# Graph attention and gated graph network, one core: the copies of the GRU's aggregates out of PSUM move from VectorE to ScalarE, and the planner makes the order anew

## The chip, the core and the metric

The kernel runs on one core of a Trainium2 chip. The metric is the device time of one execution in microseconds (us); lower is better. Before the change it is 2776.41 us, the median of 3 runs (2775.74 to 2777.18).

## The reference

There are 128 independent graphs of 128 nodes with 256 features each, all in float32. Three graph attention layers are followed by a gated graph network of three GRU steps. Every layer normalizes its input, applies a ReLU and adds its result to the input.

```python
# layers 0, 1, 2
h = relu(layernorm(x))
Wh = h @ W                                   # 256 x 256 weights
e = leaky_relu((Wh @ a1)[:, :, None] + (Wh @ a2)[:, None, :], 0.2)
att = softmax(where(adj > 0, e, -9e15), axis=-1)
x = x + elu(att @ Wh)
# layer 3, on h = relu(layernorm(x))
A = (adj != 0)
for i in range(3):
    m = h @ weight[i]
    aggr = einsum('bst,bsd->btd', A, m)      # sum over the neighbours
    gi, gh = aggr @ w_ih.T + b_ih, h @ w_hh.T + b_hh
    r = sigmoid(i_r + h_r); z = sigmoid(i_z + h_z)
    n = tanh(i_n + r * h_n)
    h = (1 - z) * n + z * h
x = x + h
```

## The kernel before, in words

**Groups.** The 128 graphs are cut into 33 groups: one of 2 graphs, 31 of 4 and one of 2 (`SIZES`). For each group `gat(g)` does the three attention layers (`attention(g, l, ...)`) and prepares the GRU, and `gru(g, ...)` does the three steps. Most tiles of a 4-graph group are 128 partitions x 512 columns.

**Attention.** For a layer, VectorE takes statistics (`bn_stats` L413, `bn_aggr` L415), GpSimd the power for the reciprocal root (L422, L424), and ScalarE makes the normalized rows `xn` (L497). VectorE forms the scores (L505), GpSimd prepares the next sum `xo` from `xt` (L516), VectorE adds and masks the scores (`em`, L547), applies the leaky ReLU (L559) and takes the row maxima (`nmx`, L561). ScalarE takes the exponentials (L565), VectorE the reciprocals (L572), scales (L576) and transposes in blocks (`tr_at`, L441); the rest of the transposition goes through DRAM by DMAs from SyncE's queue (L448, L452). TensorE multiplies (`ahp`, L617), ScalarE copies out of PSUM (`ah`, L624), TensorE multiplies with the weights (`hp`, L636), ScalarE takes the exponential (`t`, L650), and VectorE adds both parts into `xo` (L652, L654). The first two groups transpose on TensorE and not through DRAM (L536, L589).

**One GRU step.** `step(i)` has two halves `c` of 128 features. The message weights are folded with the input weights into `wc`, so that the step first sums the neighbours' states and then multiplies. `aggregate(k)`, for each half `k` of the features, multiplies the states `hn[k]` (nodes on partitions) with the adjacency `am` into the PSUM tile `agp` (L803; 4 products, one for each graph) and copies `agp` to the SBUF tile `ag[k]` (L811). `half(c)` accumulates in PSUM: `nn`, `r` and `z` from the state `h` and `whh`, then `r`, `ni` and `z` from `ag` and `wc` (all L780). ScalarE reads them: `wn` (L833), `r` (L838), `n` (L848), `z` (L853). VectorE combines them: L841, L846, `d` (L861 or L863, and L867), and the new state (L870). For the next step the new state must lie with nodes on partitions: for groups 2 to 30 `turned_state` transposes blocks on VectorE (L466) and turns them through DRAM (L469, L473); the other groups transpose on TensorE (`hnp`, L752) and copy on ScalarE (`hn`, L792).

**PSUM.** Eight banks of 128 x 512: two for attention, five for the GRU's `nn`, `r`, `z` and `ni`, and one, `tr`, for `agp`, `hnp` and `hTp`. As there is one `tr` bank, the next `agp` or `hnp` can't begin before the copy of the last has read it.

**What sets the order.** Nothing is issued where it stands in the code. Every operation goes into a `Plan` with an engine, a cost and a rank (`add`, L62). `issue` (L108) plays the program through with these costs, as a list scheduler: on each engine it takes, of the operations that could start within 0.1 us of the first, the one of lowest rank, among those within `AHEAD` = 6 ranks of the oldest operation that is still open. The order so found is fixed as the instruction order of each engine; each engine then works its list in that order and waits where an input isn't there. The costs are functions of the column count (L256 to L266): `dve` is 0.12 + cols / 1000, `act` is 0.25 + cols / 1400. Loads and stores by DMA are planned on SyncE with 0.45 us each and a landing time. The plan allows for neither a VectorE operation that is held up by GpSimd nor a DMA that lands later than planned. The rank of the GRU's element-wise work, the aggregates' copies among it, is 2 lower than its step's (`quick`, L767), so that it goes ahead of the attention's.

Of the kernel before, what the change touches and what calls it, by code (L numbers as in the profile page):

```python
# [39 lines left out]
class Plan:  # L40
# [21 lines left out]
    def add(self, engine, cost, rank, fn, reads=(), writes=(), after=(), takes=()):  # L62


        reads = [k if isinstance(k, tuple) else (k, None) for k in reads]
        writes = [k if isinstance(k, tuple) else (k, None) for k in writes]
        vals = list(dict.fromkeys(v for v, _ in reads + writes))
        vals += [v for v in dict.fromkeys(takes) if v not in vals]
        op = Op(engine, cost, rank, fn, vals)
        for v in vals:  # L70
            v.ops.append(op)

        def others(book, key):
            for part, ops in book.get(key[0], {}).items():
                if part is None or key[1] is None or part == key[1]:
                    yield from ops

        for key in reads:
            for d in others(self.writers, key):
                op.deps[d] = True  # L80
        for key in writes:
            for book in (self.writers, self.readers):
                for d in others(book, key):
                    op.deps.setdefault(d, False)
        for d in after:
            op.deps.setdefault(d, False)
        for v, part in writes:
            w, r = self.writers.setdefault(v, {}), self.readers.setdefault(v, {})
            if part is None:
                w.clear()  # L90
                r.clear()
            else:
                r.pop(part, None)
            w[part] = [op]
        for v, part in reads:
            if (v, part) not in writes:
                self.readers.setdefault(v, {}).setdefault(part, []).append(op)
        for d in op.deps:
            d.users.append(op)
        self.ops.append(op)  # L100
        return op
# [80 lines left out]
def kernel(  # L182
# [25 lines left out]
    nc = tc.nc  # L208
# [25 lines left out]
    add, load = plan.add, plan.load  # L234
# [15 lines left out]
    def bank(tag, name):  # L250
        n = BANKS[tag]
        return plan.val(
            psum, tag, n, lambda: psum.tile([P, T], FT, tag=tag, name=name, bufs=n)
        )

    def pe(cols):  # L256
        return 0.035 + cols / 600 if cols <= P else 0.01 + cols / 600

    def dve(cols):
        return 0.12 + cols / 1000  # L260

    def act(cols):
        return 0.25 + cols / 1400
# [462 lines left out]
    def gru(g, xt, am, hn0, h0):  # L726
# [3 lines left out]
        TG = n_g * N  # L730
# [17 lines left out]
        def node_major(name, hv, k, rank, to):  # L748
            ps = bank("tr", f"hnp_{name}_{k}")

            def turn(b):
                add("PE", 0.11, rank, lambda: nc.tensor.transpose(  # L752
                    ps.t[:, b * P : (b + 1) * P], hv.t[:, b * P : (b + 1) * P], ident
                ), reads=[hv], writes=[(ps, b)], takes=[to])

            for b in range(n_g):
                turn(b)
            return ps
# [4 lines left out]
        def step(i):  # L763
# [3 lines left out]
            quick = rank - URGENT  # L767
# [18 lines left out]
            def aggregate(k):  # L786

                if i > 0:
                    hv = hn[k]
                    if not through:  # L790
                        hp = node_major(name, h[k], k, rank + 0.1 * k, hv)
                        add("ACT", act(TG), quick, lambda: nc.scalar.copy(  # L792
                            hv.t[:, :TG], hp.t[:, :TG]), reads=[hp], writes=[hv])
                ps = bank("tr", f"agp_{name}_{k}")
                t = ag[k]

                def part(b):
                    def fn():
                        if i > 0:
                            s = hv.t[:, b * P : (b + 1) * P]  # L800
                        else:
                            s = hn0.t[:, b, k * P : (k + 1) * P]
                        nc.tensor.matmul(  # L803
                            ps.t[:, b * P : (b + 1) * P], s, am.t[:, b, :], start=True, stop=True
                        )
                    add("PE", pe(P), rank + 0.1 * k, fn,
                        reads=[hv if i > 0 else hn0, am], writes=[(ps, b)], after=after, takes=[t])

                for b in range(n_g):
                    part(b)  # L810
                add("DVE", dve(TG), quick, lambda: nc.vector.tensor_copy(t.t[:, :TG], ps.t[:, :TG]),  # L811
                    reads=[ps], writes=[t])

            def half(c):
# [7 lines left out]
                for k in range(KD):  # L822
                    early = rank + 0.1 * k if c == 0 else at
                    ops = [
                        product(nn, cn, whh, h[k], k, k == 0, k == KD - 1, early, takes),
                        product(pr, cr, whh, h[k], k, k == 0, False, early, takes),
                        product(pz, cz, whh, h[k], k, k == 0, False, early, takes),
                    ]
                    if k == 0:
                        begun += ops  # L830
                    if c == 0:
                        aggregate(k)
# [125 lines left out]
```

## Time and profile before

| | |
|---|---|
| median of the runs | 2776.41 us |
| profiled execution | 2774.5 us |
| its span | 2772.7 us, 32377 instructions |
| TensorE matmul busy | 2710.1 us (98%) |
| VectorE busy | 2199.0 us (79%), 5738 instructions |
| ScalarE busy | 1171.7 us (42%), 2511 instructions |
| GpSimd busy | 288.2 us (10%) |
| copies of the aggregates, L811, on VectorE | 198, 130.8 us |
| copies of `ah`, L624, on ScalarE, of the same shapes | 198, 112.9 us |

The profile was taken in an execution of its own, which is 1.9 us below the median of the runs. PE is TensorE's matmuls and PEld its weight loads, DVE is VectorE, ACT is ScalarE, POOL is GpSimd and SP is SyncE. A float32 product appears as two matmul records. The records' ends are modelled, so that the busy time of PE says how often it had work and not how fast it worked; the distance from start to start tells that. "idle before" is the time that an engine stood still ahead of an instruction, and the name after the arrow is what released it last.

### The profile page before, as it was taken

Reading aid. Unit: us, or ns where it says so; the run is one execution under the profiler, and the core shown is the slowest. Engines: PE = TensorE matmul, PEld = TensorE weight load, DVE = VectorE, ACT = ScalarE, POOL = GpSimd, SP = SyncE. Lnnn points to the kernel's source line nnn. Section 1 sums busy time; section 2 is a strip of 40 time slices with the busy share of each in tenths; the row PEclk is TensorE's granted clock in tenths of the full one; section 3 lists DMA queues with packets and bytes.
Section 4 is the critical chain, followed back from the end, with each engine's and each line's share of the span. In section 5 each row is a group of like instructions: output and inputs, shape, how many; then the busy total and the mean of one; then the engine's idle time right before and its main releaser. Section 6 shows DMA issues by size and latency. Waiting matters only on the chain.

```text
span 2772.7 us, 32377 instructions
## 1 busy us (share of the span) xinstructions
PE 2710.1 (98%) x9557; PEld 1565.2 (56%) x9557; DVE 2199.0 (79%) x5738; ACT 1171.7 (42%) x2511; POOL 288.2 (10%) x369
## 2 busy tenths in 40 slices
PE   6998999999999999999999999999999999999998
PEld 4755555555555555555555555555555555555546
DVE  7778888887888878887888878788788887888644
ACT  4444444443444444443444444444344444444322
POOL 2101011010101010101011101011101010101000
PEclk9999999999999999999999999999999999999999
DMA  3213234333334323334333334333333333333310
GB/s 102 57 44 103 77 94 110 103 86 92 89 93 111 105 75 99 91 92 111 97 83 96 95 92 107 103 84 91 88 100 103 104 87 88 80 94 93 78 44 12
DMA packets 503519, 246.08 MB, mean 89 GB/s; under 512 B 280624, under 2 KB 472112, under 8 KB 503344
## 3 DMA queue, kind: packets, MB, share of 16 engines
q1 hardware_dynamic: 503344, 244.03, 33.6%
q8 instruction: 76, 1.25, 0.2%
q14 instruction: 99, 0.81, 0.1%
HBM read 140.06 MB, written 103.87 MB: 88 GB/s over the span
## 4 chain that ended last, share of the span: by engine, by line
PE 84%; DVE 11%; ACT 2%; DMA 1%; issue 1%; SPq 0%; POOL 0%; ACTq 0%; DVEq 0%; POOLq 0%
PE r L780 21%; PE z L780 21%; PE ni L780 11%; PE hp L636 10%; PE nn L780 9%; PE ahp L617 6%; PE agp L803 5%; DVE em L547 2%; DVE xo L652 1%; DVE xo L654 1%; ACT em L565 1%; DVE ag L811 1%; DVE d L867 1%; DVE h L870 1%; DVE d L863 1%
## 5 line engine op out<-in xcount | busy, mean ns | idle before, releaser
L780 PE MATMUL nn<-h,whh 128*128 128x512 f32 (+1 forms) x792 | 396.3, 582 | 11.2 <-DMA h<-d_h 9.0
L780 PE MATMUL r<-ag,wc 128*128 128x512 f32 (+1 forms) x792 | 394.5, 581 | 8.4 <-DVE ag L811 8.4
L780 PE MATMUL r<-h,whh 128*128 128x512 f32 (+1 forms) x792 | 395.2, 580 | 0.0
L780 PE MATMUL z<-h,whh 128*128 128x512 f32 (+1 forms) x792 | 394.3, 579 | 0.0
L780 PE MATMUL z<-ag,wc 128*128 128x512 f32 (+1 forms) x792 | 394.1, 579 | 0.0
L780 PE MATMUL ni<-ag,wc 128*128 128x512 f32 (+1 forms) x792 | 394.0, 579 | 0.0
L636 PE MATMUL hp<-w,ah 128*128 128x256 f32 x1536 | 360.5, 380 | 2.5 <-ACT ah L624 2.4
L636 PEld LDWEIGHTS hp<-w,ah 128*128 128x128 f32 x1536 | 290.5, 191 | 100.7 <-issue 61.5
L841 DVE SCALAR_TENSOR_TENSOR n<-r,wn 128x512 f32<-128x512 f32 (+1 forms) x198 | 133.6, 675 | 224.8 <-ACT r L838 222.9
L505 DVE SCALAR_TENSOR_TENSOR scr<-xn,va 128x256 f32<-128x256 f32 x732 | 268.6, 419 | 32.4 <-ACT xn L497 32.2
L833 ACT ACTIVATE wn<-nn,bh 128x512 f32<-128x512 f32 (+1 forms) x198 | 132.9, 671 | 359.1 <-PE nn L780 358.9
L838 ACT ACTIVATE r<-r,brz 128x512 f32<-128x512 f32 (+1 forms) x198 | 132.8, 671 | 351.8 <-PE r L780 351.5
L803 PEld LDWEIGHTS agp<-am,hn 128*128 128x128 f32 x1536 | 201.1, 191 | 88.3 <-issue 64.1
L780 PEld LDWEIGHTS r<-ag,wc 128*128 128x128 f32 x792 | 148.3, 190 | 176.4 <-issue 145.8
L780 PEld LDWEIGHTS z<-h,whh 128*128 128x128 f32 x792 | 150.1, 190 | 170.9 <-issue 161.5
L565 ACT ACTIVATE em<-em,nmx 128x128 f32<-128x128 f32 x384 | 149.3, 390 | 228.3 <-DVE nmx L561 228.3
L780 PEld LDWEIGHTS z<-ag,wc 128*128 128x128 f32 x792 | 148.3, 190 | 159.4 <-issue 157.4
L780 PEld LDWEIGHTS r<-h,whh 128*128 128x128 f32 x792 | 147.8, 191 | 159.7 <-issue 155.0
L780 PEld LDWEIGHTS ni<-ag,wc 128*128 128x128 f32 x792 | 146.7, 190 | 154.5 <-issue 137.1
L617 PEld LDWEIGHTS ahp<-at,xn 128*128 128x128 f32 x1536 | 188.8, 194 | 47.6 <-issue 42.1
L803 PE MATMUL agp<-am,hn 128*128 128x128 f32 x1536 | 205.9, 276 | 8.7 <-ACT hn L792 4.4
L780 PEld LDWEIGHTS nn<-h,whh 128*128 128x128 f32 x792 | 138.5, 191 | 103.8 <-issue 95.0
(91 smaller groups left out, 3401.9 us busy)
## 6 DMA issues: line engine op xcount, KB each, us to landing
d_hn<-tr_hn SPq DMA_DIRECT2D x116, 256.0 KB, 2.3
hn<-d_hn SPq DMA_DIRECT2D x464, 64.0 KB, 2.4
er<-de SPq DMA_DIRECT2D x90, 256.0 KB, 3.8
d_at<-tr_at SPq DMA_DIRECT2D x90, 256.0 KB, 2.0
at<-d_at SPq DMA_DIRECT2D x360, 64.0 KB, 2.0
x<-in_x_dram SPq DMA_DIRECT2D x31, 512.0 KB, 4.0
d_h<-tr_h SPq DMA_DIRECT2D x31, 512.0 KB, 3.0
h<-d_h SPq DMA_DIRECT2D x124, 128.0 KB, 3.2
```

The source lines that it names most:

```text
L505: add("DVE", dve(D), rank, lambda: nc.vector.scalar_tensor_tensor(scr.t, xn.t[:, b, :], 1.0 if far else rs.t[:, b : b + 1], VA[l].t[:, s, ...
L547: add("DVE", dve(P) + (0.15 if far else 0.05), rank, lambda: nc.vector.scalar_tensor_tensor(em.t[:, b, :], e2_row(b), e.t[:, 0, b : b + 1] ...
L565: add("ACT", 0.42, rank, lambda: nc.scalar.activation(em.t[:, b, :], em.t[:, b, :], AF.Exp, bias=nmx.t[:, b : b + 1], accum_out=sm.t[:, b ...
L617: add("PE", pe(P), rank, lambda: nc.tensor.matmul(summed(ps, b), xn.t[:, b, k * P : (k + 1) * P], turned_weights(b), start=True, stop=True ...
L636: add("PE", pe(D), rank, lambda: nc.tensor.matmul(hp.t[:, b * D : (b + 1) * D], ah.t[:, k, c * P : (c + 1) * P], W[l].t[:, k, :], start=(k ...
L652: add("DVE", dve(T), rank, lambda: nc.vector.scalar_tensor_tensor(u(), hp.t, 0.0, u(), op0=OP.max, op1=OP.add), reads=[hp, *parts], writes ...
L654: add("DVE", dve(T), rank, lambda: nc.vector.scalar_tensor_tensor(u(), t.t, 1.0, u(), op0=OP.min, op1=OP.add), reads=[t, *parts], writes=p ...
L780: nc.tensor.matmul(o, w.t[:, k, c * P : (c + 1) * P], m, start=start, stop=stop)
L803: nc.tensor.matmul(ps.t[:, b * P : (b + 1) * P], s, am.t[:, b, :], start=True, stop=True)
L833: add("ACT", act(TG) + 0.1, quick, lambda: nc.scalar.activation(wn.t[:, :TG], nn.t[:, :TG], AF.Identity, bias=bh.t[:, cn : cn + 1]), reads ...
L838: add("ACT", act(TG) + 0.1, quick, lambda: nc.scalar.activation(r.t[:, :TG], pr.t[:, :TG], AF.Tanh, bias=brz.t[:, cr : cr + 1], scale=0.5) ...
L841: add("DVE", dve(TG), quick, lambda: nc.vector.scalar_tensor_tensor(n.t[:, :TG], r.t[:, :TG], 1.0, wn.t[:, :TG], op0=OP.add, op1=OP.mult), ...
```

## The change

The copy of `agp` into `ag` is put on ScalarE, with ScalarE's cost function in the plan. No other line differs.

```diff
                 for b in range(n_g):
                     part(b)
-                add("DVE", dve(TG), quick, lambda: nc.vector.tensor_copy(t.t[:, :TG], ps.t[:, :TG]),
+                add("ACT", act(TG), quick, lambda: nc.scalar.copy(t.t[:, :TG], ps.t[:, :TG]),
                     reads=[ps], writes=[t])
```

For 512 columns the plan's cost of the copy goes from 0.632 to 0.616 us. Since the order comes from the plan, the order of all engines is made anew from the first aggregate on: of the instruction orders of the two kernels, PE, DVE, ACT, POOL and SP agree up to there and differ in many places after it. All 198 copies stand on ScalarE in the changed kernel and none on VectorE; the number of instructions of every other kind stays as it was.

## The prediction

> **What bounds the kernel now.** I read the page first: its shares and the slices of PE.
>
> ```profile
> span 2772.7 us, 32377 instructions
> ...
> PE 2710.1 (98%) x9557; PEld 1565.2 (56%) x9557; DVE 2199.0 (79%) x5738; ACT 1171.7 (42%) x2511; POOL 288.2 (10%) x369
> ...
> PE   6998999999999999999999999999999999999998
> ```
>
> TensorE has work 98% of the time. So 130 us less on VectorE is worth nothing in itself: a gain can only come out of TensorE's 63 us without work, and out of the slow clock after a long pause. Where they lie, the table by stage shows (columns: window, length, PE busy, PEld, DVE, ACT, POOL, PE clock, DMA share, GB/s):
>
> ```profile
> 208.00:277.00 69.00, 55.30 (x214) 34.82 (x213) 55.57 (x161) 29.98 (x67) 9.05 (x12) 0.93 0.38 104
> 277.00:2634.00 2357.00, 2345.63 (x8112) 1327.84 (x8111) 1920.09 (x4949) 1004.91 (x2133) 247.44 (x308) 1.00 0.36 94
> ```
>
> The long middle has only 11.4 us of idle in 2357; the first 277 us have about 42, the last 139 about 10. What ends TensorE's waits, from its list of waits (us in total, times, longest):
>
> ```profile
> PE nn L780 <- DMA h<-d_h: 9.0, 2, 8.4
> PE r L780 <- DVE ag L811: 8.4, 14, 0.8
> ```
>
> The 14 waits for `ag` are most of the middle's 11.4. Nearly all come in pairs, one of 0.5 and one of 0.76 us, every four groups (333.7 us), the first at 395.14, the last at 2483. One of them, TensorE's timeline (start, us, engine, line, operands, idle before):
>
> ```profile
> 477.27 1.02 PE L780 MATMUL nn<-h,whh 128*128 128x512 f32 x2
> 478.13 1.02 PE L780 MATMUL r<-h,whh 128*128 128x512 f32 x2
> 479.90 1.13 PE L780 MATMUL r<-ag,wc 128*128 128x512 f32 x2 [0.76 <-DVE ag L811]
> 480.87 1.02 PE L780 MATMUL ni<-ag,wc 128*128 128x512 f32 x2
> ```
>
> A pair takes 0.86 from start to start; `r` to `r` took 1.77 (0.91 too much) and the pair after it 0.97 (0.11 too much): 1.02 us lost where 0.76 is shown. Why the copy was late, VectorE's timeline shows, and GpSimd's:
>
> ```profile
> 471.62 2.84 DVE L547 SCALAR_TENSOR_TENSOR em<-er,e,cap 128x128 f32<-128x128 f32 x4
> ...
> 477.62 0.18 DVE L572 RECIPROCAL ri<-sm 128x4 f32<-128x4 f32 x1
> 477.84 0.69 DVE L576 TENSOR_TENSOR em<-em,ri 128x512 f32<-128x512 f32 x1
> 478.56 0.71 DVE L441 STREAM_TRANSPOSE tr_at<-em 128x512 f32<-128x512 f32 x1
> 479.20 0.65 DVE L811 COPY ag<-agp 128x512 f32<-128x512 f32 x1
> ```
> ```profile
> 471.79 1.13 POOL L516 TENSOR_SCALAR xo<-xo 128x1024 f32<-128x1024 f32 x1 [21.22 <-DVE xo L654]
> 472.89 1.07 POOL L516 TENSOR_SCALAR xo<-x 128x1024 f32<-128x1024 f32 x1
> ```
>
> Four `em` instructions, 436 ns each at the median, take 2.84 us while L516 runs. The plan does not know this. Everything behind them on VectorE slides by about 1 us, and the copy comes last, though TensorE had finished `agp` before 477.4.
>
> [...]
>
> ```profile
> L624 ACT COPY ah<-ahp 128x512 f32<-128x512 f32 (+1 forms) x198 | 112.9, 572 | 194.1 <-PE ahp L617 192.3
> ...
> L811 DVE COPY ag<-agp 128x512 f32<-128x512 f32 (+1 forms) x198 | 130.8, 661 | 48.5 <-PE agp L803 48.1
> ```
>
> [...] L547 takes 343 ns at least and 1122 at most beside an L516. [...] at 220.57 a ready `ah` copy started only after an `xn` that waited for `nm` until 220.06, and TensorE stood 2.43 us. [...] after the idle of 8.43 us the first two pairs took 1.84 and 1.70 instead of 0.86.
>
> **The change, part by part.**
>
> *Busy time.* 198 copies leave VectorE: 2199.0 − 130.8 = 2068 us. ScalarE gets as many at L624's 572: 1171.7 + 113 = 1285 us (46%). Neither bounds, so no time follows from this. Each copy is 0.09 us shorter; where a copy is awaited that is gained, in the tail about 0.1 us in all (its copies are of 256 columns, 0.41 to 0.37): **−0.1**.
>
> *Removed: the 14 waits.* Lost with each, as worked out above: 7 shorter ones (idle 0.5) 0.66 + 0.11 = 0.77, together 5.4; 6 longer ones 1.02, together 6.1; the last about 0.6. All go, as the copy no longer stands behind `em`, `ri` and `tr_at`: **−12.1**. Next late behind them is nothing seen in the middle, where the other waits sum to 3 us.
>
> *Added: the copy in ScalarE's queue.* Each copy now stands behind ScalarE's `exps` (L565), `xn` (L497) or attention's `hn` (L691), which wait for VectorE's `nmx` or `nm`; and behind a waiting copy stand `wn` (L833), `exps` and `xn`, whose readers are the GRU's five PSUM banks and VectorE's `n`. By TensorE's new order I counted, for each copy, the TensorE work between the last `agp` product and the first reader of `ag`. At most 1.7 us of cover: 67 of 198 before, 66 after. Of the former 57 lie in groups 2 to 30, with 36 right behind a VectorE operation that waits for ScalarE, and 14 stalled. Of the latter about 40 stand right behind a ScalarE operation that waits for VectorE. No copy stands behind one that TensorE releases later. Where ScalarE is clear, a copy needs 0.2 (TensorE's last product to its start, as at L624) + 0.59 + 0.05 (its end to the reader, as at 479.90) = 0.84; the shortest covers are 0.86 and 1.08 and stand behind no such waiter: no stall. For the others I ran groups 12 to 16 by hand with durations of this trace, `em` stretched by 1 us wherever L516 may meet it: one copy comes 0.05 to 0.3 late, one 0.4 (1.4 if both L516 fall on it), the others fit. The new order repeats every six groups: 29 / 6 = 4.8 times 0.7 gives 3.4; bounds 4.8 × 0.45 = 2 and 4.8 × 1.7 = 8. I take **+3.5**.
>
> *Moved: the whole order.* DMAs keep their number but are issued from SP in another order. (a) `hn` turned through DRAM needs about 9.8 us; the least cover ahead of its `agp` is 11.2 in 1 case before, 14 after. The two waits of before, 0.28 and 0.44 us, came of a full SP queue. I take **+0.5** (0 to 5, if each of the 14 lost 0.35). (b) Group 2's wait for `h` (8.4 us, then 1.8 us of slow clock) is the largest single one. Its load `d_h` took 5.9 us, the median is 3.0; in the new order a load of `x` that shared the DMA engines with it is issued earlier, and TensorE's `hp` ahead of it comes 0.86 us sooner; but eight score transposes and two more transfers stand ahead of it on VectorE and SP. **−2** (−4 to +2). Smaller waits just ahead of it (1.7, 2.4, 1.2) only feed this one. (c) Group 2's next step: the wait of 1.25 + 0.2 for `h` gets 1.4 us more cover and goes; one copy there has cover 0 and costs about 1.05: **−0.4**. (d) Between 78 and 208 us the single waits, 6 us in all, change places: 0 (±2). Up to 78 us and in the tail TensorE's order is the same.
>
> Sum against the profiled execution: 2774.5 − 12.1 − 0.1 + 3.5 + 0.5 − 2 − 0.4 = 2763.9. The median lies 1.9 above the profiled: **2766 us**.
>
> **The rivals.** (1) *Stalls exchanged one for one.* The late `em` now holds `nmx`, hence `exps`, and the copy waits behind `exps` on ScalarE: the same 1 us by another road, and 12 us come back. For it: as many tight copies as before. Against: the copy now needs to wait for fewer VectorE operations, and the hand chains. 2774.5 + 1 + 1.9: 2775 to 2777. (2) *Slower.* One mechanism: of the 40 tight copies behind a ScalarE waiter, more than a third are held by an `em` stretched by GpSimd. Each costs 1.0 us; 12 of them pay the gain back, from 18 the kernel is measurably slower, and 22, with the 2 us of group 2 not won, give 2774.5 − 12.1 + 22 + 1.9 = 2786. Against: in the chains one or two copies of six groups came late, not five. (3) *More.* No new stalls and group 2 early by 4, the start better by 2: 2774.5 − 12.1 + 0.5 − 4 − 2 − 0.5 + 1.9 = 2758. (4) That the change doesn't do what it says is excluded: the instruction order has 198 copies L811 on ScalarE and none on VectorE.
>
> **How the numbers follow.** Forecast 0.66 (own range 2759 to 2771), rival 1 0.20, rival 2 0.07, rival 3 0.07. 0.2% is 5.6 us, about what a measurement of this kernel tells from no change: faster means below 2770.8. Faster: nearly all of the forecast's (0.63) and rival 3: 0.70. Same: rival 1 and the forecast's upper end: 0.23. Slower: 0.07. The range leaves out rival 2, half of rival 3 and half of rival 1's upper end: 2757 to 2776.
>
> **What would show it.** Right: L811 in ScalarE's group at about 570 ns; VectorE about 2068 and ScalarE 1285 us; no wait of `r` for a VectorE `ag`; waits for a ScalarE `ag` below 4 us in the middle, with a period of six groups; the window 277 to 2634 with less than 6 us idle; the wait for `h` near 234 us of about 6. Wrong: waits for a ScalarE `ag` of 8 us or more (rivals 1, 2), new waits for `hn` by DMA, or a group-2 wait longer than 8.4.

## The result, and the profile after

| | before | changed |
|---|---|---|
| median of five runs | 2775.74 us | 2763.23 us (2760.43 to 2764.1) |
| ratio | | 0.9954, 95% interval 0.994 to 0.9969 |
| profiled execution: span | 2772.7 us | 2761.4 us |

The changed kernel is 0.46% faster: 12.5 us by the medians, 11.3 by the two profiled executions. The page of the changed kernel, for the three rows shown of before:

```profile
span 2761.4 us, 32274 instructions
...
PE 2708.5 (98%) x9557; PEld 1567.8 (57%) x9557; DVE 2086.2 (76%) x5540; ACT 1277.0 (46%) x2709; POOL 292.5 (11%) x369
...
L811 ACT COPY ag<-agp 128x512 f32<-128x512 f32 (+1 forms) x198 | 112.9, 570 | 279.9 <-PE agp L803 279.3
```

The copies are on ScalarE and take 570 ns. VectorE fell by 112.8 and not by 130.8 us. In the main that is because a record overlaps the next: in before's timeline the copy at 479.20 is drawn 0.65 us long, but the next instruction starts after 0.57, so that a copy adds less to the busy time than its own record says. TensorE still has work 98% of the time. The stages (columns as before: window, length, PE busy, PEld, DVE, ACT, POOL, PE clock, DMA share, GB/s):

```profile
208.00:277.00 69.00, 57.34 (x216) 35.66 (x215) 53.67 (x164) 32.37 (x74) 8.89 (x12) 0.93 0.35 94
277.00:2634.00 2357.00, 2353.48 (x8151) 1334.92 (x8149) 1829.68 (x4793) 1101.47 (x2310) 252.96 (x310) 1.00 0.36 94
```

The idle time of the long middle fell from 11.4 to 3.5 us. TensorE's list of waits says what is left of those for `ag`, and beside them that for group 2's `h` (us, times, longest):

```profile
PE nn L780 <- DMA h<-d_h: 8.5, 1, 8.5
...
PE r L780 <- ACT ag L811: 1.7, 4, 0.5
...
PE agp L803 <- DMA hn<-d_hn: 1.1, 2, 0.9
...
PE ni L780 <- ACT ag L811: 0.9, 1, 0.9
```

The 14 waits for a VectorE `ag` are gone. Four shorter ones for a ScalarE `ag` stand at 725, 1223, 1723 and 2222 us, every six groups, all for the same kind of copy as the 14 of before, the second half of the third GRU step (step 2). One of them, first TensorE, then ScalarE, VectorE and GpSimd of the changed kernel (start, us, engine, line, operands, idle before):

```profile
723.72 1.02 PE L780 MATMUL nn<-h,whh 128*128 128x512 f32 x2
725.15 1.12 PE L780 MATMUL r<-ag,wc 128*128 128x512 f32 x2 [0.41 <-ACT ag L811]
```
```profile
723.53 1.09 ACT L497 ACTIVATE xn<-xo,nm,rs 128x256 f32<-128x256 f32 x2 [2.06 <-DVE nm L493]
724.53 0.56 ACT L811 COPY ag<-agp 128x512 f32<-128x512 f32 x1
```
```profile
716.19 1.45 DVE L547 SCALAR_TENSOR_TENSOR em<-er,e,cap 128x128 f32<-128x128 f32 x2
717.68 1.39 DVE L559 SCALAR_TENSOR_TENSOR em<-em 128x512 f32<-128x512 f32 x1
...
723.34 0.16 DVE L493 TENSOR_TENSOR nm<-nm,rs 128x4 f32<-128x4 f32 x1
```
```profile
716.36 1.12 POOL L516 TENSOR_SCALAR xo<-xo 128x1024 f32<-128x1024 f32 x1 [21.84 <-DVE xo L654]
717.46 1.07 POOL L516 TENSOR_SCALAR xo<-x 128x1024 f32<-128x1024 f32 x1
```

It is before's story with one more link. GpSimd's two L516 hold up `em` and then L559 (1.39 us instead of 0.69). VectorE reaches `nm` late, ScalarE's `xn` waits for it, and the copy stands behind `xn`, though TensorE had gone on from its `agp` at 722.86. At all four places an L559 takes 1.39 us and the copy stands behind such an `xn`.

**How delays are measured below.** A pair of matmul records is drawn 1.02 us long, but the next starts after 0.86. A delay is therefore shown as idle time 0.16 us too short, and one of less isn't shown at all. Where two kernels have the same TensorE order, I set the same instruction of both traces side by side and take the step in the difference of their start times. The start of the kernel differs between profiles (group 2's wait for `h` ends between 233 and 238 us), so that the table below also gives the span less the end of that wait: "from h on".

### The profile page after: what moved, and what is told of

It reads as the page before. It is cut to its first block, busy times and chain, and to the rows that moved or that the text cites. A ratio compares the mean times of both kernels' runs of the same rounds, so it can differ in the third digit from the quotient of the medians.

```text
span 2761.4 us, 32274 instructions
## 1 busy us (share of the span) xinstructions
PE 2708.5 (98%) x9557; PEld 1567.8 (57%) x9557; DVE 2086.2 (76%) x5540; ACT 1277.0 (46%) x2709; POOL 292.5 (11%) x369
## 4 chain that ended last, share of the span: by engine, by line
PE 90%; DVE 5%; DMA 2%; ACT 1%; issue 1%; SPq 1%; POOL 0%; DVEq 0%; ACTq 0%; POOLq 0%
PE r L780 22%; PE z L780 22%; PE ni L780 11%; PE hp L636 11%; PE nn L780 11%; PE ahp L617 6%; PE agp L803 6%; DMA er<-de 1%; DVE scr L505 1%; DVE st L413 0%; DVE em L547 0%; DVE xo L654 0%; DVE xo L652 0%; DVE h L870 0%; DVE d L867 0%
## 5 line engine op out<-in xcount | busy, mean ns | idle before, releaser
L636 PE MATMUL hp<-w,ah 128*128 128x256 f32 x1536 | 369.5, 381 | 0.2 <-ACT ah L624 0.2
L841 DVE SCALAR_TENSOR_TENSOR n<-r,wn 128x512 f32<-128x512 f32 (+1 forms) x198 | 133.3, 673 | 309.8 <-ACT r L838 309.1
L811 ACT COPY ag<-agp 128x512 f32<-128x512 f32 (+1 forms) x198 | 112.9, 570 | 279.9 <-PE agp L803 279.3
L617 PE MATMUL ahp<-at,xn 128*128 128x128 f32 x1536 | 190.9, 277 | 2.0 <-DMA at<-d_at 1.2
```

What stands on the lines that cost most here:

```text
L617: add("PE", pe(P), rank, lambda: nc.tensor.matmul(summed(ps, b), xn.t[:, b, k * P : (k + 1) * P], turned_weights(b), start=True, stop=True ...
L636: add("PE", pe(D), rank, lambda: nc.tensor.matmul(hp.t[:, b * D : (b + 1) * D], ah.t[:, k, c * P : (c + 1) * P], W[l].t[:, k, :], start=(k ...
L811: add("ACT", act(TG), quick, lambda: nc.scalar.copy(t.t[:, :TG], ps.t[:, :TG]), reads=[ps], writes=[t])
L841: add("DVE", dve(TG), quick, lambda: nc.vector.scalar_tensor_tensor(n.t[:, :TG], r.t[:, :TG], 1.0, wn.t[:, :TG], op0=OP.add, op1=OP.mult), ...
```

## The experiments

The line L811 has two parts: the engine and cost that the plan is told, and the instruction that is issued. They can be set apart. Each median stands against that of before measured beside it (2776.6 to 2777.1 us; 2775.7 for the changed kernel), and the interval is that of their ratio.

| kernel | median, us | ratio (95%) | from h on, us |
|---|---|---|---|
| before | 2776.6 | 1 | 2536.6 |
| changed | 2763.2 | 0.994 to 0.9969 | 2525.4 |
| ScalarE copy, before's order | 2759.9 | 0.9927 to 0.9952 | 2520.7 |
| VectorE copy, changed order | 2797.6 | 1.0062 to 1.0087 | 2559.3 |
| before, L516 without reading | 2760.7 | 0.9929 to 0.9954 | 2525.2 |
| changed, L516 without reading | 2755.7 | 0.9911 to 0.9938 | 2521.8 |
| only step 2's second half on ScalarE | 2764.4 | 0.9941 to 0.9966 | 2525.1 |
| all but these on ScalarE | 2766.7 | 0.9949 to 0.9976 | 2528.0 |
| VectorE copy planned at 0.616 | 2777.4 | 0.9993 to 1.001 | 2538.3 |
| ScalarE copy planned at 0.55 | 2763.3 | 0.9939 to 0.9966 | 2526.0 |
| ScalarE copy planned at 0.70 | 2764.2 | 0.9943 to 0.9968 | 2527.1 |
| changed, longer `em` in the plan | 2767.0 | 0.9953 to 0.9978 | 2530.0 |
| before, longer `em` in the plan | 2817.4 | 1.0129 to 1.0157 | 2577.1 |
| ScalarE copy, group 2's `h` on TensorE | 2759.5 | 0.9926 to 0.9951 | |

### The engine alone, the order alone

```diff
-                add("DVE", dve(TG), quick, lambda: nc.vector.tensor_copy(t.t[:, :TG], ps.t[:, :TG]),
+                add("DVE", dve(TG), quick, lambda: nc.scalar.copy(t.t[:, :TG], ps.t[:, :TG]),
```

> The copy L811 is on ScalarE, but the plan still takes it for a VectorE operation of the old cost, so TensorE, SP and GpSimd have before's order row for row. Theory (the copy no longer queues behind em, ri and tr_at on VectorE): the 14 waits of r for ag at 395, 480, 729, ... are gone, about 12 us less than before, 2762 to 2766 us. Rival (the new order is what brings the gain, the engine does not matter): within 3 us of before, 2773 to 2779, with waits for ag in the same 14 places.

2759.9 us: 16.7 less than before, more than the whole change brings and 2 us below the theory's own range. The middle is nearly without a gap:

```profile
277.00:2634.00 2357.00, 2355.38 (x8162) 1337.72 (x8162) 1836.53 (x4798) 1108.78 (x2313) 253.05 (x310) 1.00 0.36 94
```

1.6 us of idle are left of 2357. TensorE's order is before's, so each step can be read off. From 298 us on the same instructions come some 16.3 us sooner at the end. The 14 waits give 12.1 of it: 0.65 + 0.11 for each of the seven shorter, 0.92 + 0.11 for each of the six longer, 0.49 + 0.10 for the last. The other 4 us are three waits for `hn` at 362, 975 and 2310 us (1.6 together), one of 0.46 at 2637, and six times 0.36 at the second `agp` of step 0 (665, 999, 1333, ... us). Of the first four, before's list of waits has 1.2 us; the six show in no list. The first of the six, in before and then here:

```profile
664.04 1.02 PE L780 MATMUL nn<-h,whh 128*128 128x512 f32 x2
665.16 1.16 PE L803 MATMUL agp<-am,hn 128*128 128x128 f32 x8
666.15 1.02 PE L780 MATMUL r<-h,whh 128*128 128x512 f32 x2
```
```profile
661.97 1.02 PE L780 MATMUL nn<-h,whh 128*128 128x512 f32 x2
662.83 1.05 PE L803 MATMUL agp<-am,hn 128*128 128x128 f32 x8
663.72 1.02 PE L780 MATMUL r<-h,whh 128*128 128x512 f32 x2
```

It is 1.12 us from `nn` to `agp` in before and 0.86 here, and 0.99 against 0.89 after it. The `agp` wanted the one `tr` bank, which VectorE's copy of the first `agp` (664.42 to 665.10, behind `d`, `d` and `h`) had yet to empty. No idle time is printed there.

```diff
-                add("DVE", dve(TG), quick, lambda: nc.vector.tensor_copy(t.t[:, :TG], ps.t[:, :TG]),
+                add("ACT", act(TG), quick, lambda: nc.vector.tensor_copy(t.t[:, :TG], ps.t[:, :TG]),
```

> The copy L811 is on VectorE, in the order that the plan made for a ScalarE copy: TensorE, SP and GpSimd as in the changed kernel row for row. Theory (engine): the copies stand behind em again, waits of r for a VectorE ag in 8 or more places of the middle, 2771 to 2782 us. Rival (new order): 2761 to 2766 us, as the changed kernel, with at most five waits for ag in the middle.

2797.6 us, 21 more than before. The theory's direction holds and its size was too small:

```profile
PE r L780 <- DVE ag L811: 20.8, 20, 2.3
```

There are 20 waits, up to 2.3 us, in an order whose plan thought VectorE free of these copies. So the two parts of the change have opposite signs. The engine is worth 16.7 us in before's order and 34 in the new one. The order made anew costs 21 with VectorE's copies and 3 to 5 with ScalarE's (2763.2 against 2759.9 by the medians, 2525.4 against 2520.7 from h on; the intervals of the two ratios overlap, so that the second is shown by one trace of each rather than by the medians).

### Is it GpSimd?

```diff
-        add("POOL", 0.14 + n * D / 1070, rank, lambda: nc.gpsimd.tensor_scalar(
-            xo.t, xt.t, 1.0, -1.0, op0=OP.mult, op1=OP.add), reads=[xt], writes=[xo])
+        add("POOL", 0.14 + n * D / 1070, rank, lambda: nc.gpsimd.memset(
+            xo.t, -1.0), reads=[xt], writes=[xo])
```

> The kernel before, but GpSimd's L516 fills xo with -1 in place of reading xt (the residual of the attention layers is left out); all orders on the other engines are before's. Theory (em is held up by GpSimd's read): em near 0.35 to 0.45 us everywhere, none above 0.6, the 14 waits for ag gone, 2762 to 2766 us. Rival (VectorE's queue is simply too full for the copy, the GpSimd collision is incidental): em shorter, but waits for ag stay in at least 8 of the 14 places, 2770 to 2776 us.

2760.7 us, a little below the theory's range. No `em` is long any more (min/median/max in ns; 1122 at most in before):

```profile
L547 DVE SCALAR_TENSOR_TENSOR em<-er,e,cap x366: 343/436/465, 92.2 to 2636.0; 128x128 f32<-128x128 f32 x183
```

The 14 waits are gone with the copies still on VectorE and in before's order; by the steps they give 12.1 us, the same as when the copies left VectorE. Two separate cures of one delay have the same worth. So GpSimd's L516 beside `em` is the cause.

Is it that L516 reads, or only that GpSimd is at work? The fill doesn't wait for `xt` and mostly runs at other times than L516 (447.8 to 449.6 instead of beside `em`), so the time alone doesn't tell. But some fills do meet VectorE. In this run and the next, as far as GpSimd's rough spans tell, 34 operations with both inputs in SBUF (`em`, L576, L654 and the GRU's L841, L863, L867 and L870) start while a fill runs, and none takes over 0.70 us, no longer than without one. In before seven such operations, `em` not counted, start while an L516 runs, and they take 0.72 to 1.56. The two `em` among the 34 are the first two of these four, in the next run, VectorE and GpSimd:

```profile
228.75 1.48 DVE L547 SCALAR_TENSOR_TENSOR em<-er,e,cap 128x128 f32<-128x128 f32 x4 [1.34 <-DMA er<-de]
```
```profile
228.60 0.95 POOL L516 MEMSET xo<- 128x1024 f32 x1
```

The four `em` take 1.48 us here, and 2.84 beside an L516 that reads. So these operations are held up beside the L516 that reads, and not beside the fill. That a fill holds up nothing on VectorE is not shown: the small `nm` (L420, 128x4) at 475.67 us in the first of the two runs took 0.58 us beside one, and 0.17 at most in before.

Of the 15.9 us between the medians the two profiles have 13.8, of which 1.9 lie ahead of 298 us, where profiles differ among themselves; the other 2 are in no trace.

> The changed kernel with the same fill in place of L516 (the residual of the attention layers is left out). Theory: its four waits for ag of 0.4 to 0.5 us, every 498 us, go too, as the xn or exps ahead of the copy is no longer late: 2 us less than the changed kernel, 2759 to 2763 us, so that the whole change is worth at most 4 us once GpSimd's read is gone. Rival: the four waits stay, 2762 to 2765 us.

2755.7 us, 7.5 below the changed kernel where 2 were expected. The four waits for `ag` went (2.8 us with what follows them) and, with them, parts of waits for `hn`: 3.6 from h on. The other 3 come from the first 236 us, and the single profiles differ by as much there, so that I leave them open. Against the kernel before with the same edit the change is worth 5.0 us instead of some 13: most of its worth is that it takes the copy out of the reach of GpSimd's collision.

### Which copies

```diff
-                add("DVE", dve(TG), quick, lambda: nc.vector.tensor_copy(t.t[:, :TG], ps.t[:, :TG]),
+                add("DVE", dve(TG), quick, lambda: (nc.scalar.copy if i == 2 and k == 1 else nc.vector.tensor_copy)(t.t[:, :TG], ps.t[:, :TG]),
```

The second run has `not (i == 2 and k == 1)` in its place.

> Before's order; only the copies of the second half (k = 1) of the third GRU step, 33 of 198, are on ScalarE. All 14 waits of r for ag of before are of these copies. Theory: those 14 are the main term, 12.0 us by the distance of the same TensorE instructions in two traces, so 2763 to 2766 us against 2776.6. Rival (the gain is spread over all copies by VectorE's lower load): about a sixth of 16.7, 2772 to 2775 us.

> Before's order; the other 165 copies are on ScalarE and the 33 of the run beside it stay on VectorE. Theory: what is left of 16.7 after the 14 waits, about 4 us, comes from the second agp of step 0 of every fourth group, which waits for the bank of the first (6 times 0.36) and from three waits for hn: 2771 to 2774 us, and the 14 waits for ag are there again, perhaps a little shorter as VectorE has 109 us less to do. Rival (VectorE's load as a whole delays the copy): the 14 waits shrink to less than half, 2764 to 2768 us.

33 copies bring 12.8 us, as expected: a sixth of the copies and three quarters of the gain. The other 165 bring 10.5, where I expected 4; 2766.7 us lies in the rival's range and not in the theory's. The sum is 23 and not 16.7, so they share some 6.6 us. The trace of the second run shows where, at the wait of 479.90 in before:

```profile
478.64 1.02 PE L780 MATMUL r<-h,whh 128*128 128x512 f32 x2
479.82 1.13 PE L780 MATMUL r<-ag,wc 128*128 128x512 f32 x2 [0.16 <-DVE ag L811]
```

The copy of the second half is still on VectorE and still late, by 0.32 us instead of 0.91. The copy of the first half (469.83 in before) had stood ahead of `em` in the same queue, and its 0.6 us are gone. So the lateness is a sum along VectorE's queue, 0.6 for one copy and 1.4 for GpSimd (2.84 against 1.49 where nothing disturbs the four `em`), and the copy comes 0.91 too late. Taking out the first part alone earns 0.6 of the 0.91, the second alone all of it, and both together no more than the 0.91. At the shorter waits the first part alone earns less, 0.28 of 0.65. By the steps the 14 waits shrink by 6.0 us in this run, from 12.1, which is most of the shared part. So the rival was half right: I read it as not VectorE's load as such, but what of it stands ahead of the copy.

### Luck of the order, and what the plan knows

```diff
-                add("DVE", dve(TG), quick, lambda: nc.vector.tensor_copy(t.t[:, :TG], ps.t[:, :TG]),
+                add("DVE", act(TG), quick, lambda: nc.vector.tensor_copy(t.t[:, :TG], ps.t[:, :TG]),
```

> The copy stays on VectorE, but is planned at 0.616 instead of 0.632 us, so that the plan, and a third of TensorE's order, come out anew. A control for the luck of an order. Theory: no gain of the size of the change comes from an order alone, 2770 to 2785 us, with waits for a VectorE ag of 6 us or more. Rival (luck of the order): 2760 to 2767 us.

2777.4 us, no change, with the waits for `ag` in the same 14 places:

```profile
PE r L780 <- DVE ag L811: 8.1, 14, 0.8
```

As a control it is weaker than expected. By line and tile name, row by row in the two traces, TensorE's sequence differs from before's at 254 of 9557 places, of which 120 lie behind the first 200 us; that of the changed kernel differs at 3028. (The names carry no buffer numbers, so that two like rows that change places don't count.) In the middle this is nearly before's own order. It shows that the small change of the cost does nothing; that no other order with VectorE's copies could bring the gain is not shown.

The changed kernel with `act(TG) - 0.066` and `act(TG) + 0.084` in the plan:

> The changed kernel with the ScalarE copy planned at 0.55 instead of 0.616 us: a new order, a fifth of TensorE's rows of which differ. Theory (the 3.4 us between the changed kernel and the run with ScalarE's copies in before's order are the luck of one order): 2758 to 2766 us, on either side of 2763.2. Rival (a plan that puts the copy on ScalarE is worse by its nature): 2763 to 2770 us, with four or more waits of r for a ScalarE ag.

> The same with the copy planned at 0.70 us; nearly all of the order is new. Theory (luck): 2757 to 2766 us, and not on the same side of 2763.2 by the same amount as the run beside it. Rival (by nature): 2763 to 2770 us.

2763.3 and 2764.2 us, within 1 us of the changed kernel, each with four or five waits of `r` for `ag`, nearly all in a period of six groups. The first is no new order, though: behind the first 200 us TensorE's rows differ from the changed kernel's at 8 places. The second is, with 3418 rows that differ. So two orders planned for ScalarE came out alike. That is no support for my theory of luck, but two are too few to refute it, and both times lie in its ranges as well as in the rival's. Why before's order does better I can only argue: it keeps 0.63 us of VectorE's time for a copy that isn't there, which is a cushion for the late `em`.

```diff
-            add("DVE", dve(P) + (0.15 if far else 0.05), rank, lambda: nc.vector.scalar_tensor_tensor(
+            add("DVE", dve(P) + (0.40 if far else 0.05), rank, lambda: nc.vector.scalar_tensor_tensor(
```

In the two expectations that follow, the planned cost is 0.65 instead of 0.40 us for one `em`, all told. That is nearer the truth only for those that meet L516: in before's trace 43 of the 366 `em` take over 0.6 us, and the median is 0.44.

> The changed kernel with each em (L547) of groups 2 on planned at 0.50 instead of 0.40 us above its columns' share, that is 0.25 us more, 1.0 us for four, which is what GpSimd's read costs it. Theory (the four waits for ag come from a plan that doesn't know of that): they are gone or below 0.2 us in sum, 2758 to 2762 us. Rival (the longer costs only shift the order; other waits come in): 2762 to 2768 us.

2767.0 us, in the rival's range. The four waits went as the theory had it, and others came as the rival had it: from 400 us to 2590 TensorE has two waits over 0.15 us, of 0.19 and 0.24, and none for `ag`. But between 352 and 400 us, in groups 3 and 4, six new ones sum to 4.65 us, for `h`, `hn` and the `tr` bank.

> The kernel before, copies on VectorE, with the same longer cost of em in the plan. Theory (a plan that knows the true length of em puts the copy ahead of em, or TensorE work between): most of the 14 waits are gone without moving any copy, 2763 to 2770 us. Rival (VectorE's queue is too full for any order): 2772 us or more.

2817.4 us, 41 more than before. The theory was wrong, and of the rival only "2772 or more" came true, not its cause. All 14 waits for `ag` are gone. In their place:

```profile
PE agp L803 <- DMA hn<-d_hn: 35.0, 14, 3.8
```

One of them, on TensorE and on SP's queue (second column: time in issuing):

```profile
470.20 1.02 PE L780 MATMUL r<-ag,wc 128*128 128x512 f32 x2
474.52 1.77 PE L803 MATMUL agp<-am,hn 128*128 128x128 f32 x8 [3.30 <-DMA hn<-d_hn]
476.08 1.91 PE L780 MATMUL z<-ag,wc 128*128 128x512 f32 x2
```
```profile
462.55 2.72 SPq L452 DMA_DIRECT2D h<-d_h  x4
...
465.84 0.38 SPq L469 DMA_DIRECT2D d_hn<-tr_hn  x1
470.42 1.91 SPq L473 DMA_DIRECT2D hn<-d_hn  x4
```

VectorE had `tr_hn` ready at 463.5. SP was then issuing the four loads of `h`, and `d_hn`, at last issued at 465.84, ran beside those and `er`, issued just ahead of it: it took 4.6 us to landing instead of 2.4. That the others slowed it is my reading of this order. The plan gives each DMA 0.45 us of SP and a landing time of its own, whatever runs beside it.

The wait costs more than it shows, as TensorE is slower behind it: the `agp` takes 1.56 us from start to start instead of 0.89, the pair behind it 1.70 instead of 0.86 and the next 1.09, so that 5.2 us are lost where 3.30 are shown. Behind group 2's wait of 8.43 us in before, where the first two pairs took 1.84 and 1.70, the granted clock is 0.50 from 236.1 to 239.6 us. The mean granted clock of this run's executions is 0.986 to 0.989, of before's beside it 0.994 to 0.996. Counted in this way the 14 waits lose 56 us for the 35 shown. With before's 12.1 and some smaller waits saved, that is nearly all of the 41.

### A faster version?

The engine alone is already faster than both kernels. I added to it what took the largest single wait away, group 2's `h`, by turning it on TensorE:

```diff
-        if g == 0:
+        if g in (0, 2):
             for k in range(KD):
                 turned(k)
```

> Copies on ScalarE, planned as VectorE's (as in the first experiment, 2760 us), and the first state h of group 2 is turned on TensorE, as group 0's is, not through DRAM; the order is new from group 1 on. Theory: the wait of 8.4 us for group 2's h and 1.8 us of slow clock after it shrink to less than 3, for 1 us more of TensorE work: 2750 to 2755 us. Rival: another late input takes the wait's place (the transposed weights of group 3, or hn of group 2), or the new order brings stalls of its own: 2757 to 2765 us.

2759.5 us, the same as without it. This is what the rival said. The wait of 8.4 is gone, but TensorE meets other inputs that aren't there: nine waits from 261 to 557 us, 0.3 to 1.7 each, 8.9 us in all, for `h`, `hn` and one `ag`. My reading is that the wait had given the groups after it a lead; as the order is new from group 1 on, the runs don't show this by itself.

## Why the prediction was right, step by step

The forecast was 2766 us and the measured time is 2763.2, inside the likeliest case's own range. Between the profiled executions 10.6 us were forecast and 11.3 came. Of the 2.8 us between the medians 1.9 are the step from the profiled execution to the median: it was added because before's profile lay that far below its median, but the changed kernel's profiled execution is its median. That the sum came within 0.7 us is in part luck: a term of −2 did not come and one of −2.7 that was not in the sum did.

- **The 14 waits, −12.1.** Right: two cures gave 12.1 each. The cause given, `em` beside L516, is shown. The stretch itself was put at about 1 us and is 1.4.
- **What the lists don't show, 0 in the sum.** The sum had no term for waits under 0.16 us. Six waits of `agp` for its bank (0.36 each, 2.2 us) and one of 0.46 near 2637, which the list shows as 0.2, went too: −2.7.
- **The copy in ScalarE's queue, +3.5.** Four new waits cost 2.8. The mechanism and the period of six groups were right, the count was not: one copy in six groups is late, by 0.6 to 0.7, where I had worked out two, of at most 0.3 and of 0.4. I had stretched `em` alone; in the late one the second L516 falls on L559.
- **`hn` by DMA, +0.5.** Three waits, at 1302, 1801 and 2300 us, 1.4 us of idle in TensorE's timeline and 1.8 with the 0.16 that each hides, against 1.5 in before: +0.3.
- **Group 2's `h`, −2.** It did not come. The wait was to be about 6 and is 8.5 us, and it ends at 236.04 us, in before at 236.10. `d_h` did land after 2.9 us instead of 5.9, with the load of `x` issued at 216.24 and not at 224.65, but the four loads of `h` took 4.9 to 5.3 us instead of 2.6 to 3.1. The way from the end of the wait for `nm` (67.1 and 69.7 us) to its end is 2.6 us shorter than in before (166.4 against 169.0), but that shows no gain: among the runs with before's TensorE order it varies from 167.1 to 169.0, and with the changed order from 165.9 to 169.5.
- **Groups 2 and 3, −0.4.** Right in kind: the waits at 297 and 299 us went (2.0 with what they hide and what follows) and one at 268 came (0.90 shown, 1.2 with what it hides and what follows): −0.8.
- **The tail, −0.1.** From the first wait for `hn` there to the last product it is 85.57 us in both: 0.
- **The rivals.** The first, one for one, came true in a quarter of its size (2.8 of 12), by `xn` behind `nm` and not by `exps` behind `nmx`. The second, slower, did not. The third, more, did not either: new stalls came, and group 2 was not early.

From h on, −12.1 + 2.8 + 0.3 − 0.8 − 2.7 makes −12.5; the traces differ by −11.2. Of the 1.3 us between, some 1.0 are waits of the changed order that show almost no idle time: from start to start TensorE loses 0.3 at 1362, 0.4 at 2518 and 0.3 at 2589 us. The rest is not placed.

## What to carry to other kernels

Where a planner makes the order, a change of engine is two changes: issue the instruction on the new engine in the old order, and on the old one in the new order, before either is believed. A cost raised to what an operation takes at its worst doesn't make a truer plan, as long as most of these operations are shorter and the plan's queues and landing times are not true either (41 us slower here). And a wait at the end of an in-order queue is a sum along that queue: cures of its parts do not add up (12.8 and 10.5 us apart, 16.7 together). Before an order made anew is taken for a control, count how much of it is new.

## What was not expected of the hardware

- After a short idle spell the first pair of products takes 0.96 to 0.97 us from start to start instead of 0.86, even after 0.2 us (725.15, 2624.66 us in the changed kernel); such a wait costs 0.1 more than itself. After one of 3.3 us (474.52, in the kernel before with the longer `em` in the plan) it cost 1.7 more than the delay itself: the first two steps took 1.56 and 1.70 us instead of 0.89 and 0.86.
- A GpSimd operation that only fills held up none of 34 VectorE operations with both inputs in SBUF (0.70 us at most), while beside L516, which reads, four `em` took 2.84 us instead of 1.49 and an L559 1.39 instead of 0.69. The small L420 took 0.58 us beside a fill.
- 256 KB from SBUF to DRAM in blocks (`d_hn`, 465.84 us in the kernel before with the longer `em` in the plan) took 4.6 us beside the loads of `h` and `er`, against 2.4 at the median.
